# W_up for two pairs: 26 quarter-block products in place of seven half-block ones

## The chip, the cores and the metric

The kernel runs on one core of a Trainium2 chip. TensorE (PE) multiplies matrices into PSUM, eight banks of 512 f32 values for each of 128 partitions; VectorE (DVE), ScalarE (ACT) and GpSimd (POOL) work element by element, and SyncE (SP) issues DMAs. The metric is the device time of one execution in microseconds, as a median over runs.

## The reference

Input x is 128 samples of 64 channels by 1024 positions, f32. Two residual layers:

```python
x = x + ffn0(cond0(x))       # cond0: a 64x64 channel mix per sample, mixed from 8 kernels by an attention
                             # ffn0: out = in @ (A @ B.T).T + bias, rank 128
y = cond1(x)                 # grouped convolution over 1024 positions, 9 taps, 4 groups, plus a context
logits = y @ gate_w.T + expert_bias        # 4 experts
base   = einsum("bth,oh->bto", y, W_up)    # 1024 x 1024: most of the arithmetic
delta  = one_hot(argmax(logits)) picks one of 4 rank-8 LoRA products of y
x = x + base + delta
```

The 8192 rows (128 samples x 64 channels) each take a 1024 x 1024 product with `W_up`, all in f32.

## The kernel before

**Tiling.** Two samples make a *pair*: 128 rows by 1024 columns, tile `x` (64 pairs). Two pairs make a *group* `d` (32 groups), pair a = 2d and pair b = 2d+1. The convolution's result comes out transposed, as `yt` (128 positions by [2 pairs, 8 chunks, 128 rows]), so a 128x128 piece of `yt` is the stationary matrix of a matmul and a piece of `W_up` the moving one. PSUM: a pool `ps` of four banks (tags `bank`) for all small steps, and four banks `pb0` to `pb3` for W_up.

**W_up before.** With a0, a1 (b0, b1) the halves of pair a (b) along the 1024 inputs, and 11, 12, 21, 22 the four 512x512 blocks of W_up, seven block products do for eight. `product()` (L459) makes one: four matmuls of 512 columns. `ffn_sums` (L478) makes four sums of `yt` blocks on POOL; `w_sum` (L137) makes T1, T2, T3, -T4 from the weight blocks once, on DVE. `ffn_a` (first product, copied to SBUF as `v` by ACT), `ffn_second`, `ffn_both`, `ffn_b`, `ffn_hi` and `ffn_last` make the products; DVE makes `u2`, `u3` out of PSUM (L549, L558), POOL adds them to `x` (L550, L551, L559), DVE adds T1's product to `x` (L564). `lora` (L586) puts the four expert results onto the open banks and one bank `pl`; `results` (L594) adds them to `x` with four DVE additions, and SP stores the two `x` tiles.

**Order.** All five engines run in the order in which the program names the work (a manual schedule); waits on semaphores are put in from the data. For group d of the main loop (L735) PE does: `layer0_out(2d+5)` (two matmuls `pd` of 512 columns, added to `x` by DVE at L353; `x` goes through DRAM, `x1d`, and comes back as `X`), `gate` (L506, matmul `pgt`, then eight small DVE operations L514 to L526), the last five products of group d with `turn` (`pzt`) among them, then `tiles`: `shared_in` (`pm`), `gate_in` (`pg`, for group d+1), `conv_in` (`pc`, for group d+2), `lora`; then `layer0_in` of the two pairs 2d+6 and 2d+7 (`pxb`), `layer0_mix` (`pz`), the first product of group d+1, `layer0_out(2d+6)`, `layer0_mix`, the second product. So the `yt` that group d+1 needs was complete one turn earlier.

**POOL's order** in a turn: `add_fbias` of two pairs (L603), the three additions to `x`, `differences` of two pairs (L389, L390), the loads of two later pairs (`load_x`, two DMAs each, L108, L109), then `ffn_sums(d+1)`.

**The start.** Before the loop, lines L636 to L734 do the conditioning, load the weights (L673 to L677), run pairs 0 to 5 through layer 0 and group 0's products up to `ffn_hi`, with the weight sums between them:

```python
gate_out(0, gate_in(0)); ffn_sums(0); add_fbias(4, nc.gpsimd)      # L700 to L702
ffn_a(0); layer0_in(4)
w_sum("T1", "12", "11"); w_sum("T2", "22", "T1"); w_sum("T3", "22", "12")
```

Of the kernel before, what the change touches and what calls it, by code (L numbers as in the profile page):

```python
# [52 lines left out]
E, R = 4, 8  # L53
ER = E * R
GL = E + ER
HC = NC // 2
H = P // 2
N = 512
GT = 64
NX = 3  # L60
NBD = 3
FIRST = 4
PLAIN = 2

PK = tuple(np.cumsum([0, P, P, 1, 1, P, 8, 8, CH, CH, E]).tolist())

# [2 lines left out]
def block(ctx: ExitStack, tc: tile.TileContext, a: dict, out: bass.AP):  # L69
# [21 lines left out]
    def bank(name):  # L91
        return ps.tile([P, 512], F32, tag="bank", name=name)
# [35 lines left out]
    load_x(0, nc.sync)  # L128
    at = loaded("AT", [P, L])
    wk = loaded("wk", [P, 8, 2, CH], eng=nc.scalar)  # L130
    W = {}

    def load_w(name, eng, tag=None):
        W[name] = const.tile([P, HC, N], F32, tag=tag or f"w{name}", name=f"w{name}")
        eng.dma_start(W[name], a[f"w{name}"])

    def w_sum(name, x, y):  # L137
        W[name] = const.tile([P, HC, N], F32, tag=f"w{name}", name=f"w{name}")
        nc.vector.tensor_tensor(W[name], W[x], W[y], ALU.subtract)


    X = []
# [110 lines left out]

    def own_bias(pr):

        mv[pr] = const.tile([8, 2, CH], F32, name=f"mv{pr}")
        for b in range(2):
            nc.scalar.activation(mv[pr][:, b], bk, AF.Copy, scale=attT[:8, 2 * pr + b : 2 * pr + b + 1])

    def own_bd(pr):  # L260
        bdx[pr] = const.tile([P, 2, CH], F32, name=f"bdx{pr}")
        for k in range(8):
            w = attx[pr][:, k : k + 1]
            if k == 0:
                nc.vector.tensor_scalar(bdx[pr], wk[:, k], w, None, ALU.mult)
            else:
                nc.vector.scalar_tensor_tensor(bdx[pr], wk[:, k], w, bdx[pr], ALU.mult, ALU.add)  # L267
# [22 lines left out]
    def agg_all():  # L290

        to = aggd.rearrange("b i o -> b (i o)").rearrange("b (j h n) -> h b j n", j=4, h=2)
        for h in range(2):
            pool, tag = ((const, "wT3"), (ytp, "yt"))[h]
            agg = pool.tile([NB, 4, 512], F32, tag=tag, name=f"agg{h}")
            aggs.append((to[h], agg))
            ps4 = [spare(j, f"pagg{h}_{j}") for j in range(4)]
            for j in range(4):
                rows = slice(32 * j, 32 * (j + 1))
                nc.tensor.matmul(ps4[j], attT[rows, :], wa[rows, h], start=True, stop=True)  # L300
            for j in range(4):
                if j % 2:
                    nc.scalar.copy(agg[:, j], ps4[j])
                else:
                    nc.vector.tensor_copy(agg[:, j], ps4[j])
            yield

    def agg_out():
# [3 lines left out]

    lo, hi = slice(0, N), slice(N, L)
    xbs, z0s, yts, opened = {}, {}, {}, {}
    diffs, pms, m2s, pcs, zgs, vs, ss, u2s = {}, {}, {}, {}, {}, {}, {}, {}

    def layer0_in(pr):
        xt = xts.pop(pr)
# [137 lines left out]
            conv_in(pr, b)  # L456
            conv_out(pr, b)

    def product(to, yt, w, first=True):  # L459

        for c in range(HC):
            nc.tensor.matmul(  # L462
                to, yt[:, c], w[:, c], start=first and c == 0, stop=c == HC - 1, skip_group_check=not first
            )

    def halves(d):

        yt = yts[d]
        return [[yt[:, t, h * HC : (h + 1) * HC] for h in range(2)] for t in range(2)]

    def ffn_a(d):

        opened[d] = [psb.tile([P, N], F32, tag=f"pb{i}", name=f"pb{i}_{d}") for i in range(4)]
        product(opened[d][0], halves(d)[0][0], W["11"])
        vs[d] = sums.tile([P, N], F32, tag="v", name=f"v{d}")
        nc.scalar.copy(vs[d], opened[d][0])

    def ffn_sums(d):  # L478
        (a0, a1), (b0, b1) = halves(d)
        s = [sums.tile([P, HC, P], F32, tag=f"s{i}", name=f"s{i}_{d}") for i in range(4)]  # L480
        nc.gpsimd.tensor_tensor(s[0], b0, b1, ALU.add)
        nc.gpsimd.tensor_tensor(s[1], s[0], a0, ALU.subtract)
        nc.gpsimd.tensor_tensor(s[2], a0, b0, ALU.subtract)
        nc.gpsimd.tensor_tensor(s[3], a1, s[1], ALU.subtract)
        ss[d] = s

    def gate_in(d):

# [49 lines left out]
        nc.scalar.copy(zt, p[:, :P])  # L538
        return zt

    def ffn_second(d):
        product(opened[d][0], halves(d)[0][1], W["21"], False)

    def ffn_both(d):

        xa, xb = xs[2 * d], xs[2 * d + 1]
        product(opened[d][1], ss[d][1], W["T2"])
        u2s[d] = sums.tile([P, N], F32, tag="u2", name=f"u2_{d}")
        nc.vector.tensor_tensor(u2s[d], opened[d][1], vs.pop(d), ALU.add)  # L549
        nc.gpsimd.tensor_tensor(xa[:, hi], xa[:, hi], u2s[d], ALU.add)  # L550
        nc.gpsimd.tensor_tensor(xb[:, lo], xb[:, lo], u2s[d], ALU.add)  # L551

    def ffn_b(d):

        xb = xs[2 * d + 1]
        product(opened[d][2], ss[d][2], W["T3"])
        u3 = sums.tile([P, N], F32, tag="u3", name=f"u3_{d}")
        nc.vector.tensor_tensor(u3, opened[d][2], u2s.pop(d), ALU.add)  # L558
        nc.gpsimd.tensor_tensor(xb[:, hi], xb[:, hi], u3, ALU.add)  # L559

    def ffn_hi(d):
        xb = xs[2 * d + 1]
        product(opened[d][3], ss[d][0], W["T1"])
        nc.vector.tensor_tensor(xb[:, hi], opened[d][3], xb[:, hi], ALU.add)  # L564

    def ffn_last(d, zm):
        p, s = opened[d], ss.pop(d)
        zt = turn(d, zm)
        product(p[2], halves(d)[1][1], W["-T4"], False)
        product(p[3], s[3], W["22"], False)  # L570
        del yts[d]
        return zt

    def ffn(d):

        zm = gate(d)
        ffn_both(d)
        if 2 * d + 4 < NPAIR:
            differences(2 * d + 4)
        ffn_b(d)  # L580
        if 2 * d + 5 < NPAIR:
            differences(2 * d + 5)
        ffn_hi(d)
        return ffn_last(d, zm)

    def lora(d, zt):  # L586

        p = opened[d]
        p.append(bank(f"pl{d}"))
        for j, i in enumerate((0, 3, 2, 4)):  # L590
            rows = slice(j * ER, (j + 1) * ER)
            nc.tensor.matmul(p[i], zt[rows, :], lb[rows, :], start=i == 4, stop=True, skip_group_check=i < 4)  # L592

    def results(d):  # L594
        p = opened.pop(d)
        xa, xb = xs.pop(2 * d), xs.pop(2 * d + 1)
        for x, cols, part in ((xa, lo, p[0]), (xa, hi, p[3]), (xb, lo, p[2]), (xb, hi, p[4])):
            nc.vector.tensor_tensor(x[:, cols], part, x[:, cols], ALU.add)  # L598
        nc.sync.dma_start(out[2 * d], xa)
        nc.sync.dma_start(out[2 * d + 1], xb)  # L600

# [68 lines left out]
    load_context(1)  # L670
    gl = loaded("gl", [P, NC, GT], eng=nc.scalar)
    lb = loaded("lb", [P, N], eng=nc.scalar)
    layer0_out(1, lambda: load_w("11", nc.sync))  # L673
    load_x(4, nc.sync)
    load_w("21", nc.sync)
    load_w("12", nc.sync, tag="w-T4")
    load_w("22", nc.sync)  # L677
    wsum = const.tile([P, NGC, P], F32, tag="sel", name="wsum")
    nc.gpsimd.tensor_tensor(wsum, ws[:, :, 0], ws[:, :, 1], ALU.add)
    add_fbias(3, nc.gpsimd)  # L680
# [17 lines left out]
    conv(1)  # L698

    gate_out(0, gate_in(0))  # L700
    ffn_sums(0)
    add_fbias(4, nc.gpsimd)  # L702
    ffn_a(0)
    layer0_in(4)
    w_sum("T1", "12", "11")
    w_sum("T2", "22", "T1")
    w_sum("T3", "22", "12")
    ffn_second(0)
    zm = gate(0)
    ffn_both(0)  # L710
    ffn_b(0)
    differences(2)
    layer0_mix(4)
    layer0_out(4, lambda: load_x(6, nc.sync))
    w_sum("-T4", "21", "T2")
    ffn_hi(0)
    add_fbias(5, nc.gpsimd)
    differences(3)
    layer0_in(5)
    layer0_mix(5)  # L720
    back5 = layer0_out(5, lambda: load_x(7, nc.sync), later=True)
    shared_in(2)
    back5()
    shared_in(3)
# [10 lines left out]
    for d in range(NPAIR // 2):  # L735
        more = d + 1 < NPAIR // 2
        ahead = [pr for pr in (2 * d + 6, 2 * d + 7) if pr < NPAIR]
        if d and 2 * d + 5 < NPAIR:
            layer0_out(2 * d + 5)
        if 2 * d + 5 < NPAIR:  # L740
            load_context(d + 2)
        if ahead:
            load_cond(d + 3)
        for pr in ahead:
            add_fbias(pr, nc.gpsimd)
        if d:
            zt = ffn(d)
        else:
            differences(4)
            differences(5)  # L750
            zt = ffn_last(0, zm)
        tiles(d, zt, 2 * d + 4, 2 * d + 5)
        for pr in (2 * d + 8, 2 * d + 9):
            if pr < NPAIR:
                load_x(pr)
        if more:
            ffn_sums(d + 1)
        for pr in ahead:
            layer0_in(pr)
        if ahead:  # L760
            layer0_mix(ahead[0])
        if more:
            ffn_a(d + 1)
        if ahead:
            layer0_out(ahead[0])
            layer0_mix(ahead[1])
        if more:
            ffn_second(d + 1)


def _by_rows(v):
# [101 lines left out]
```

## Time and profile before

| | |
|---|---|
| median of 3 runs (lowest, highest) | 1336.34 us (1336.19, 1337.31) |
| the profiled execution's own time | 1338.59 us |
| its span | 1336.8 us, mean granted TensorE clock 0.998 |
| busy | PE 1317.1 us (99%), weight loads 759.3, POOL 616.5 (46%), DVE 552.8 (41%), ACT 139.0 (10%) |
| DMA | 189.37 MB, 142 GB/s |

A matmul in f32 shows as two records, so 512 columns are `x2`. Records of PE overlap each other (their mean duration is longer than their spacing); the time that one takes in a stream is read from the chain of waits, which gives the length of a stretch and the records in it. POOL and DVE records are durations of single instructions. The page's engine shares are means over a start of some 100 us, 30 equal turns and an end of some 60 us with less in it.

### The profile page before, as it was taken

Reading aid. Unit: us, or ns where it says so; the run is one execution under the profiler, and the core shown is the slowest. Engines: PE = TensorE matmul, PEld = TensorE weight load, DVE = VectorE, ACT = ScalarE, POOL = GpSimd, SP = SyncE. Lnnn points to the kernel's source line nnn. Section 1 sums busy time; section 2 is a strip of 40 time slices with the busy share of each in tenths; the row PEclk is TensorE's granted clock in tenths of the full one; section 3 lists DMA queues with packets and bytes.
Section 4 is the critical chain, followed back from the end, with each engine's and each line's share of the span. In section 5 each row is a group of like instructions: output and inputs, shape, how many; then the busy total and the mean of one; then the engine's idle time right before and its main releaser. Section 6 shows DMA issues by size and latency. Waiting matters only on the chain.

```text
span 1336.8 us, 18273 instructions
## 1 busy us (share of the span) xinstructions
PE 1317.1 (99%) x7303; PEld 759.3 (57%) x7303; DVE 552.8 (41%) x978; ACT 139.0 (10%) x310; POOL 616.5 (46%) x541
## 2 busy tenths in 40 slices
PE   8899999999999999999999999999999999999997
PEld 6565565655665555665555655555656556656543
DVE  6652443433443423444424434324434334434222
ACT  2010111110111010111000111101111101111100
POOL 2465534455443455443555343555343555435321
PEclk9999999999999999999999999999999999999999
DMA  9965544345544455534455434455444455433301
GB/s 313 317 158 169 152 142 134 106 137 167 151 137 123 108 152 167 149 122 128 106 167 153 153 126 113 127 167 152 142 134 107 136 167 152 142 119 96 78 32 63
DMA packets 183845, 189.37 MB, mean 142 GB/s; under 512 B 17361, under 2 KB 156625, under 8 KB 183249
## 3 DMA queue, kind: packets, MB, share of 16 engines
q1 hardware_dynamic: 166480, 125.81, 33.7%
q0 software_dynamic: 16128, 58.73, 13.2%
q10 hardware_dynamic: 1152, 3.67, 0.8%
q8 instruction: 58, 0.95, 0.3%
q14 instruction: 27, 0.21, 0.1%
HBM read 118.90 MB, written 69.27 MB: 141 GB/s over the span
## 4 chain that ended last, share of the span: by engine, by line
PE 96%; DVE 2%; DMA 1%; issue 0%; ACT 0%; SPq 0%; DVEq 0%; ACTq 0%
PE pb L462 58%; PE pxb L321 9%; PE pd L352 8%; PE pc L435 8%; PE pm L397 4%; PE pg L493 4%; PE pb L592 2%; PE pz L331 1%; PE pgt L511 1%; DMA x<-in_x 1%; DVE bdx L267 1%; DMA xt<-in_xt 0%; DVE yt L447 0%; PE pc L426 0%; PE pzt L536 0%
## 5 line engine op out<-in xcount | busy, mean ns | idle before, releaser
L462 PE MATMUL pb<-wT,s 128*128 128x512 f32 x768 | 337.6, 596 | 0.0
L109 POOL DMA_DIRECT2D x<-in_x x56 | 29.5, 528 | 494.9 <-DVE z L339 428.2
L462 PEld LDWEIGHTS pb<-wT,s 128*128 128x128 f32 x768 | 143.5, 190 | 168.4 <-issue 168.4
L462 PE MATMUL pb<-w,yt 128*128 128x512 f32 x512 | 230.8, 593 | 3.1 <-DVE x L598 1.7
L353 DVE TENSOR_TENSOR x<-pd,x 128x512 f32<-128x512 f32 x128 | 88.4, 691 | 236.4 <-PE pd L352 235.9
L412 DVE TENSOR_TENSOR m<-pm,cx 64x512 f32<-64x512 f32 x124 | 85.4, 689 | 219.4 <-PE pm L397 216.5
L603 POOL TENSOR_TENSOR x<-x,ffn_bias 128x1024 f32<-128x1024 f32 x62 | 146.8, 2387 | 34.2 <-DMA x<-in_x 34.2
L462 PEld LDWEIGHTS pb<-w,yt 128*128 128x128 f32 x512 | 92.4, 190 | 98.6 <-issue 92.2
L321 PEld LDWEIGHTS pxb<-B,xt 128*128 128x128 f32 x1024 | 119.8, 195 | 25.2 <-DVE yt L447 22.0
L447 DVE TENSOR_TENSOR yt<-pc,m 128x512 f32<-128x512 f32 x124 | 121.3, 1099 | 20.8 <-ACT m L415 20.1
L352 PE MATMUL pd<-AT,z 128*128 128x512 f32 x256 | 122.4, 599 | 5.2 <-DVE yt L447 1.8
L321 PE MATMUL pxb<-B,xt 128*128 128x128 f32 x1024 | 125.6, 281 | 0.0
L462 PE MATMUL pb<-w-T,yt 128*128 128x512 f32 x256 | 115.2, 592 | 0.0
L462 PE MATMUL pb<-w,s 128*128 128x512 f32 x256 | 115.1, 592 | 0.0
L435 PE MATMUL pc<-ws,df 128*64 128x128 f32 x1984 | 113.6, 273 | 0.0
L435 PEld LDWEIGHTS pc<-ws,df 128*64 128x64 f32 x1984 | 110.4, 137 | 4.3
L550 POOL TENSOR_TENSOR x<-x,u 128x512 f32<-128x512 f32 x32 | 40.4, 1264 | 144.6 <-DVE u L549 144.6
L415 ACT COPY m<-m 64x512 f32<-64x512 f32 x124 | 76.5, 617 | 265.4 <-DVE m L412 261.9
L352 PEld LDWEIGHTS pd<-AT,z 128*128 128x128 f32 x256 | 48.2, 191 | 65.3 <-issue 57.4
L462 PEld LDWEIGHTS pb<-w,s 128*128 128x128 f32 x256 | 48.6, 190 | 61.2 <-issue 61.2
L462 PEld LDWEIGHTS pb<-w-T,yt 128*128 128x128 f32 x256 | 46.2, 190 | 54.8 <-issue 54.8
L397 PEld LDWEIGHTS pm<-wsum,X 128*64 128x64 f32 x992 | 53.7, 138 | 23.5 <-issue 23.5
(110 smaller groups left out, 1136.0 us busy)
## 6 DMA issues: line engine op xcount, KB each, us to landing
x1d<-x SPq DMA_DIRECT2D x128, 256.0 KB, 3.4
X<-x1d SPq DMA_DIRECT2D x128, 256.0 KB, 4.3
out<-x SPq DMA_DIRECT2D x64, 512.0 KB, 2.6
xt<-in_xt POOLq DMA_DIRECT2D x56, 512.0 KB, 4.5
x<-in_x POOLq DMA_DIRECT2D x56, 512.0 KB, 4.1
cx<-ctxd SPq DMA_DIRECT2D x32, 128.0 KB, 4.3
w<-in_w SPq DMA_DIRECT2D x4, 1024.0 KB, 9.5
ab<-aggbd SPq DMA_DIRECT2D x30, 128.0 KB, 3.2
```

Source lines behind the costliest of these rows:

```text
L321: nc.tensor.matmul(pxb[:, :P], xt[:, c, :], bt[:, c, :], start=(c == 0), stop=(c == NC - 1))
L352: nc.tensor.matmul(pd, z0, at[:, cols], start=True, stop=True)
L353: nc.vector.tensor_tensor(x[:, cols], pd, x[:, cols], ALU.add)
L397: nc.tensor.matmul(pm[b * H : (b + 1) * H, g * P : (g + 1) * P], blocks(pr, b, g, 1), wsum[:, g], start=True, stop=True,)
L412: nc.vector.tensor_tensor(by_group(m2[half, b]), by_group(pm[half]), context(pr, b, half), ALU.add)
L415: nc.scalar.copy(m2[other, b], m2[half, b])
L435: nc.tensor.matmul(pc[o * H : (o + 1) * H, cols], diffs[pr][:, 2 * g + b, o], ws[:, g, o], start=True, stop=True,)
L447: nc.vector.tensor_tensor(yt.rearrange("m q (o g two) -> m two g q o", two=2, g=NGC)[:, b], by_group(pcs.pop((pr, b))), context(pr, b) if ...
L462: nc.tensor.matmul(to, yt[:, c], w[:, c], start=first and c == 0, stop=c == HC - 1, skip_group_check=not first)
L493: nc.tensor.matmul(pg[rows, : 2 * P].rearrange("m (t r) -> m t r", t=2), gl[:, c, :], yt[:, :, c], start=c < 2, stop=c >= NC - 2,)
L550: nc.gpsimd.tensor_tensor(xa[:, hi], xa[:, hi], u2s[d], ALU.add)
L603: eng.tensor_tensor(xs[pr], xs[pr], fbias, ALU.add)
```

## The change

W_up for a group is now computed by another bilinear algorithm. `yt` of the two pairs is cut into eight blocks (2 pairs x 4 quarters of the inputs, two chunks of 128 each), W_up into 16 blocks of 256 inputs x 256 outputs, and the results into eight *parts* of 256 columns: part r is half r % 2 of bank `pb{r // 2}`, and results part r belongs to pair r // 4, columns 256 (r % 4). Thirty-two block products would be the plain way; here 26 do, named P0 to P25 below in the order of `PRODUCTS`. A product is two matmuls of 256 columns.

Before them, 17 sums of `yt` blocks are made for every group, on POOL (s0 to s16, by `Y_SUMS`, 256 columns each), and 31 sums of weight blocks once, on DVE (by `W_SUMS`, 512 columns each, in place in 26 slots). A row of `PRODUCTS` is (part, `yt` block or sum, weight slot, flag of the first matmul in a bank, number of weight sums that must be made by then, what is done with the part after the product). Values are handed from part to part, while the part goes on accumulating: "copy" is an ACT copy from PSUM into PSUM, with the sign; "add" is an ACT copy to SBUF (`v`) and a DVE addition into PSUM; "dcopy" is a DVE copy in PSUM; "x" is a DVE addition of the part to (or subtraction from) the `x` tile. A group has 14 "x", three "add", one "dcopy" and six "copy". PE waits for hand-ons by whole banks.

POOL no longer adds to `x`. `lora` uses the four open banks and no fifth; `results` adds in the order pb1, pb3, pb2, pb0, and SP issues the stores as before, pair a's ahead of pair b's. In the loop, the products of group d+1 are P0 to P3 and P4 to P7 where the first and second product stood, and P8 to P22, `turn`, P23 to P25 follow the gate; `differences` come ahead of all products; `ffn_sums(d+1)` stands before `load_x` on POOL. At the start, `add_fbias(4)` comes before `ffn_sums(0)`, and the 31 weight sums are spread over group 0's products. Some small tiles share memory with others (`agg0` becomes two tiles and two stores).

```diff
-HC = NC // 2
+QC = NC // 4
+NQ = N // 2
+Y_SUMS = (
+    (4, "+", 5), (0, "-", 8), (9, "+", 1), (2, "-", 10), (4, "-", 7), (0, "-", 12), (3, "-", 13),
+    (2, "+", 14), (6, "-", 15), (16, "-", 5), (12, "-", 15), (17, "-", 18), (11, "-", 8), (20, "-", 19),
+    (21, "+", 7), (7, "-", 13), (21, "+", 3),
+)
+W_SUMS = (
+    (10, 8, "-", 10), (16, 10, "-", 6), (17, 4, "n", 16), (2, 2, "-", 6), (18, 11, "-", 15),
...
+)
+PRODUCTS = (
+    (2, 6, 8, 1, 0, (("copy", 0, "-"),)),
+    (4, 10, 17, 1, 3, (("x", 4, "+"),)),
+    (6, 11, 16, 1, 3, (("copy", 1, "+"),)),
+    (2, 12, 2, 0, 4, (("x", 6, "+"),)),
+    (6, 2, 19, 0, 6, (("add", 0, "+"),)),
+    (5, 8, 3, 0, 7, (("add", 4, "-"),)),
+    (3, 17, 21, 0, 10, (("x", 7, "+"), ("x", 1, "+"))),
+    (0, 15, 18, 0, 11, (("x", 7, "+"),)),
+    (5, 5, 1, 0, 12, (("x", 7, "-"),)),
+    (7, 8, 10, 0, 15, ()),
+    (7, 19, 5, 0, 15, (("x", 1, "+"), ("x", 5, "+"))),
+    (2, 13, 20, 0, 16, (("x", 2, "+"),)),
+    (1, 20, 6, 0, 16, (("x", 2, "-"),)),
+    (4, 9, 22, 0, 17, (("add", 2, "-"),)),
+    (6, 18, 15, 0, 17, (("copy", 7, "-"), ("copy", 3, "-"))),
+    (1, 21, 23, 0, 18, (("copy", 6, "-"),)),
+    (4, 1, 7, 0, 19, (("x", 1, "-"), ("x", 3, "+"))),
+    (2, 0, 24, 0, 21, (("dcopy", 4, "+"), ("x", 0, "+"))),
+    (6, 22, 9, 0, 22, (("x", 5, "-"),)),
+    (0, 14, 25, 0, 23, (("copy", 2, "+"),)),
+    (4, 23, 0, 0, 25, ()),
+    (6, 7, 4, 0, 27, ()),
+    (1, 10, 10, 0, 27, ()),
+    (1, 24, 13, 0, 28, ()),
+    (7, 16, 11, 0, 30, ()),
+    (2, 3, 12, 0, 31, ()),
+)
...
+        for r, u, w, new, _, then in PRODUCTS[first:end]:
+            p = part(d, r)
...
+            for c in range(QC):
+                nc.tensor.matmul(
+                    p, ys[d][u][:, c], W[:, w, c], start=new == 1 and c == 0, stop=c == QC - 1, skip_group_check=True
+                )
+            for kind, to, op in then:
...
+                elif kind == "add":
+                    copy = sums.tile([P, NQ], F32, tag="v", name=f"v{d}_{to}")
+                    nc.scalar.copy(copy, p)
+                    combine(nc.vector, part(d, to), part(d, to), op, copy)
...
     gate_out(0, gate_in(0))
+    add_fbias(4, nc.gpsimd)
     ffn_sums(0)
...
+    def first_products(n):
+        end = done[0] + n
+        w_sums(PRODUCTS[end - 1][4])
+        products(0, done[0], end)
...
+    first_products(4)
     layer0_in(4)
+    first_products(4)
     zm = gate(0)
+    first_products(4)
     layer0_mix(4)
     layer0_out(4, lambda: load_x(6, nc.sync))
     add_fbias(5, nc.gpsimd)
+    differences(2)
+    first_products(4)
+    layer0_in(5)
     differences(3)
+    first_products(3)
     layer0_mix(5)
     back5 = layer0_out(5, lambda: load_x(7, nc.sync), later=True)
+    first_products(3)
...
         if d:
+            products(d, 8, 23)
...
+        zt = turn(d, zm)
         if d:
+            products(d, 23, 26)
...
         tiles(d, zt, 2 * d + 4, 2 * d + 5)
+        if more:
+            ffn_sums(d + 1)
         for pr in (2 * d + 8, 2 * d + 9):
             if pr < NPAIR:
                 load_x(pr)
...
         if more:
+            products(d + 1, 0, 4)
         if ahead:
             layer0_out(ahead[0])
             layer0_mix(ahead[1])
         if more:
+            products(d + 1, 4, 8)
```

## The prediction

> **What bounds the kernel now.** I read the page's busy times first, then the chain of waits through one turn of the loop, then the rows of single instructions, then the timeline of the start and the end.
>
> ```profile
> PE 1317.1 (99%) x7303; PEld 759.3 (57%) x7303; DVE 552.8 (41%) x978; ACT 139.0 (10%) x310; POOL 616.5 (46%) x541
> PE 96%; DVE 2%; DMA 1%; issue 0%; ACT 0%; SPq 0%; DVEq 0%; ACTq 0%
> ...
> 640.95 10.38 PE pb L462 x24
> 651.33 0.11 PE pzt L536
> 651.44 6.87 PE pb L462 x16
> 658.31 1.90 PE pm L397 x32
> 660.21 1.73 PE pg L493 x16
> ...
> 666.50 3.77 PE pxb L321 x32
> 670.27 0.22 PE pz L331 x2
> 670.50 3.44 PE pb L462 x8
> 673.93 1.72 PE pd L352 x4
> 675.65 0.22 PE pz L331 x2
> 675.87 3.44 PE pb L462 x8
> ```
>
> TensorE is never idle in this turn; each piece begins where the last ends, and W_up (`pb`) takes 10.38 + 6.87 + 3.44 + 3.44 = 24.13 us of 41. So a turn shortens by what PE saves, as long as nobody else comes late. Idle PE is found only in the start (the windows up to 80 us) and the end.
>
> **Loop: the products.** Removed per group: 56 records of 512 columns, 24.13 us (430 ns each). Added: 26 x 2 matmuls = 104 records of 256 columns. The nearest row is `pg`, the only one that streams 256 columns: 16 records, two of them at a time side by side, 1.73 us, so 216 ns per step. 104 x 216.25 ns = 22.49 us: 1.64 us saved a group, 50.8 us over the 31 groups of the loop. Its weights are 64 wide, here they are 128 wide. With 128 wide weights the trace has 128 columns (`pxb`, 3.77/32 = 117.8 ns) and 512 (430 ns); the line between them gives 222 ns at 256, 23.08 us, 1.05 us a group, 32.5 us. Half a 512-record, 215 ns, gives 22.36 us, 54.9 us. I take 216, since `pxb` shows loads and streams together passing every 118 ns, far inside 216; 222 and 215 stay as ends.
>
> The Trainium skill speaks against it: "TensorE: Matmul & The Clock Gate", Part 3, The mechanism, lets a weight load overlap a running matmul only where the row groups differ, and its section on LDWEIGHTS gives 107 ns for 128 columns. All row groups are used here, so by that rule, an estimate from that page, a record costs 213 + 107 ns and the change loses 3.4 us a group, 105 us in all. The 430 ns spacing of the 512-column records contradicts it.
>
> **Loop: the hand-ons.** Each value handed on is a wait of PE for ACT or DVE. What one costs in the open is shown at the end of the run, where PE had nothing else:
>
> ```profile
> 1302.73 1.89 DVE L598 TENSOR_TENSOR x<-pb,x 128x512 f32<-128x512 f32 x3 [9.16 <-PE pl L592]
> 1303.48 3.70 PE L462 MATMUL pb<-w,yt 128*128 128x512 f32 x8 [0.77 <-DVE x L598]
> ...
> 1307.22 0.58 ACT L476 COPY v<-pb 128x512 f32<-128x512 f32 x1 [5.15 <-PE pb L462]
> 1307.86 3.70 PE L462 MATMUL pb<-w,yt 128*128 128x512 f32 x8 [0.68 <-ACT v L476]
> ```
>
> The bracket is PE's idle time: 0.68 us through ACT, 0.77 through DVE, for 512 columns. For 256, an ACT copy falls from 0.585 to 0.361 (`zg`, L504), so 0.46; a DVE operation out of PSUM takes 0.691 for 512 columns (L353) and 0.344 for 128 (L339), on the line between them 0.46, so 0.55. The tables leave at least two products, 1.73 us, between a hand-on and its use: P0 to P3, P12 to P15, P13 to P16, P17 to P20, P18 to P21, P19 to P22 by one engine, P4 to P7 by both (1.01). All stay under 1.73 with 0.7 or more over. The queue ahead of P4's addition: DVE's `z` would end at 676.63 and `v` come at 677.15, so nothing is before it. No PSUM-to-PSUM copy is in the trace: bounds 0.36 and 0.585 (the 512 row), still covered. Price taken: 0; in the open, ten such hand-ons would be 5 us a group.
>
> One queue is nearer. P8's subtraction stands on DVE behind the eight gate operations, and P13 waits for its bank, 5 x 0.865 = 4.33 us after `pgt`. The gate takes 2.2 us at 681.4; in the turn shown it took 4.1, because one 8-column operation lasted 2.27 us (minimum 0.166, means 0.65 and 0.36 for L518 and L519). Then P13 is 0.2 us late. I put 1.5 us for all turns (0 to 9, a 0.3 in each).
>
> **Loop: DVE, ACT, POOL, queues.** DVE gets 18 operations of 0.46 for three of 0.69: +6.2 us a turn, 41% to about 56%, hidden in its idle time before L353 and L412 (236 and 219 us). ACT gets some 3.1 us more, 10% to 18%. POOL: a 256-column sum is 0.70 us (1.264 for 512, 2.387 for 1024), 17 make 11.9, in place of 5.3 + 3.8: +2.8 us. s2 must wait for P22 of the group before; from there PE has P23 to P25, `pm`, `pg`, `pc`, `lora`, `pxb`, `pz` and P0, some 15.8 us to P1; fifteen sums at 0.70 to 0.78 take 11.7. Hidden; if POOL came late, each us would be on PE's path. `load_x` is moved behind the sums: its `x` loads wait for the store of an earlier pair anyhow (POOL idles 17.2 us there, until 671.1), and the stores come 1.2 us later, since the first now waits for the fourth addition of `results`, not the second. The bias additions and `differences` queued behind these loads have a turn of slack. X for `pm` lands at 645.4 + 4.3 = 649.7, `pm` starts near 656.7: 7 us left. Zero for all of these.
>
> **The start.** Here DVE is on the path.
>
> ```profile
> 49.81 2.27 DVE L139 TENSOR_TENSOR wT<-w,w 128x2048 f32<-128x2048 f32 x1
> 50.05 3.17 POOL L481 TENSOR_TENSOR s<-yt 128x512 f32<-128x512 f32 x1 [15.83 <-DVE yt L447]
> 51.90 3.70 PE L462 MATMUL pb<-w,yt 128*128 128x512 f32 x8
> 52.12 3.24 DVE L139 TENSOR_TENSOR wT<-w,wT 128x2048 f32<-128x2048 f32 x1
> 53.29 3.20 POOL L482 TENSOR_TENSOR s<-s,yt 128x512 f32<-128x512 f32 x1
> ```
>
> A POOL sum that takes 1.27 us elsewhere takes 3.2 here, and DVE's 3.24: SBUF-to-SBUF operations of the two take turns. So a weight sum of 512 columns is 2.27/4, about 0.6 us, and 0.6 + 0.75 = 1.35 while POOL makes its sums. 31 weight sums are 18.6 us bare, against four that measured 11.4. Laid out by these rows: P0 at 52 as now; P1 waits for s2 (53.8), P3 for s4 (56.0); `pxb` to 58.8; sums 5 to 11 alternate with POOL and end at 66.8, P7 at 68.3; gate, with POOL's bias addition in the way, to 73; five weight sums to 76; P11 ends at 78.2; `pz`, `pd` and DVE's additions to 81.7; two sums, P15 ends at 85; four sums in `pxb`'s shadow, P18 at 89.5; second `pd` 92.2; five sums to 96.1, P21 at 97.1. `pm` and `pc` then end at 102.5, the convolution's DVE additions 2.5 us later, the last four sums at 107.4, P25 at 108.7. Before, group 0 was done at 92.2: **+16.5 us**. Ends: the bare extra DVE time less PE's own gain, +5; all 31 at 1.35, 42 - 11.4 - 1.6 = +29.
>
> **The end.** Both stores follow the fourth addition: +0.3 for the issue, up to 1.3 if two 512 KB stores share the engines (2.6 us each): +0.7. The first banks' waits in the last groups (0.77 + 0.68) stay about the same.
>
> **Sum.** -50.8 + 1.5 + 16.5 + 0.7 = -32.1 us. The profiled execution took 1338.59 us with a span of 1336.8; it lies 2.25 over the median. I carry the difference to the median: 1336.34 - 32.1 = 1304.
>
> **Rivals.**
> *Hand-ons in the open.* Many short waits, if PSUM-to-PSUM operations or the bank waits are slower than their rows. For: none such was ever run here. Against: 0.7 us to spare. At 0.5 us a group: 1304 + 15.5 = 1320.
> *Slower: weight loads stick out.* A load lasts 190 ns and now has 216 instead of 430 to hide in. For: 26 ns over. Against: `pxb`'s 118. The gain is used up by the start at a record of (24.13 - 0.60)/104 = 226 ns. At 236 ns W_up takes 24.54: 31 x 0.41 + 18.7 = +31, 1368.
> *A cheap start.* If DVE gets ahead of POOL: +5, 1293.
> *A dear start with records of 222 ns:* -32.5 + 29 + 2.2, 1335.
>
> **How the numbers follow.** Forecast 0.60 (its own range 1295 to 1312); hand-ons in the open 0.17 (1312 to 1333); cheap start 0.07; dear start and slow records 0.04 (half of it inside 0.2%, 2.7 us, about what can be told from no change); weight loads or POOL late, slower, 0.12. The range 1289 (54.9 saved, start +8) to 1334 leaves out the slower case and little else. Faster 0.84, same 0.03, slower 0.13.
>
> **What would show it.** Right: a turn of 39.7 us in the chain, products of P8 to P22 as one stretch near 12.98 us (x60), PE without idle in the loop, the first `tiles` of the loop some 16 us later, DVE near 56% and POOL near 53%. Wrong: PE waits on ACT or DVE at the product line, records over 222 ns, a loop in which POOL's s sums release PE, or a start that costs under 8 or over 25 us.

## The result and the profile after

The changed kernel takes 1313.06 us (median; 1312.16 to 1314.66) beside 1336.82 us of the kernel before on the same chip: a ratio of 0.9823, with a 95% interval of 0.9806 to 0.984. The forecast was 1304, its range 1289 to 1334. The profiled execution took 1312.86 us with a span of 1311.1, 25.7 less than the span of before. Two marks split these 25.7 into three stretches: the start of `pm` for pairs 4 and 5, where group 0 is done, and the end of the last `lora`:

| stretch, us | before | after | difference | predicted |
|---|---|---|---|---|
| span's start to `pm` of pairs 4, 5 | 92.22 | 114.51 | +22.3 | +16.5 |
| from there to the end of the last `lora` | 1238.1 | 1188.9 | -49.2 | -49.3 |
| from there to the span's end | 6.45 | 7.7 | +1.2 | +0.7 |
| sum | | | -25.7 | -32.1 |

From the page of the kernel after, the busy times, the granted clock over the span, the chain by engine and the two rows of W_up's matmuls:

```profile
PE 1275.2 (97%) x8839; PEld 1054.2 (80%) x8839; DVE 734.3 (56%) x1485; ACT 226.2 (17%) x566; POOL 727.9 (56%) x861
...
PEclk9889999999999999999999999999999999999999
...
PE 93%; DVE 3%; DMA 2%; issue 0%; ACT 0%; SPq 0%; DVEq 0%; ACTq 0%
...
L538 PE MATMUL pb<-w,s 128*128 128x256 f32 x2432 | 562.9, 382 | 12.1 <-DVE w L196 9.1
...
L538 PE MATMUL pb<-w,yt 128*128 128x256 f32 x896 | 229.6, 385 | 8.0 <-DMA w<-in_wq 2.6
```

PE is still the bound, but for 97% of the span. Weight loads rose from 759 to 1054 us, DVE from 41% to 56%, and all that PE idles at W_up's line (12.1 and 8.0 us) is small against 1275. The clock digit drops in the second and third slices, at 33 to 98 us. From the chain of waits of the kernel after, one turn (start, length, what):

```profile
643.06 0.37 PE pgt L583 x4
643.43 13.03 PE pb L538 x60
...
656.57 2.59 PE pb L538 x12
...
671.34 3.46 PE pb L538 x16
...
676.74 3.46 PE pb L538 x16
...
682.27 7.85 PE pb L538 x36
```

Every piece, those left out here too, is PE's and begins where the last one ends: none of the ten hand-ons of a group holds it. The products take 13.03 + 2.59 + 3.46 + 3.46 = 22.54 us instead of 24.13: 104 records at 217 ns, 1.59 us saved a group, and 31 x 1.59 = 49.3. A turn is 682.27 - 643.43 = 38.84 us. The waits of PE in the kernel after (who waited for whom: us in total, times, longest), first from 46 to 115 us, then, the last line, from 115 us to the end:

```profile
PE pb L538 <- DVE w L196: 11.6, 7, 3.5
PE pb L538 <- DVE w L194: 3.6, 3, 1.9
PE pb L538 <- DMA w<-in_wq: 2.6, 1, 2.6
...
PE pb L538 <- DVE x L623: 2.1, 4, 1.0
```

So PE waits for the weight sums in the start (15.2 us in ten waits), and in the 1196 us behind it only 2.1 us, where a group's first records wait for the `results` of the one before at the end of the run. The timeline of the start (start, length, engine, line, instructions in it; the bracket is idle time before it and who ended it):

```profile
69.43 7.77 DVE L196 TENSOR_TENSOR w<-w 128x512 f32<-128x512 f32 x5
69.62 2.70 POOL L629 TENSOR_TENSOR x<-x,ffn_bias 128x1024 f32<-128x1024 f32 x1 [7.74 <-DMA x<-in_x]
70.26 2.05 PE L538 MATMUL pb<-w,yt 128*128 128x256 f32 x4 [2.56 <-DVE w L196]
72.28 1.49 POOL L450 TENSOR_TENSOR df<-X 128x512 f32<-128x512 f32 x1
...
75.81 4.87 PE L538 MATMUL pb<-w,s 128*128 128x256 f32 x12 [3.50 <-DVE w L196]
...
107.68 4.44 DVE L196 TENSOR_TENSOR w<-w 128x512 f32<-128x512 f32 x4
```

Five weight sums take 7.77 us where POOL adds a bias and makes differences beside them, the last four 4.44. The x12 row behind the 3.50 us wait (P9 to P11) lasts 4.87 us, where twelve records of the loop take 2.59 by the chain. The chain of waits of the start holds this stretch and two more like it, P1 to P3 and P24 with P25:

```profile
54.72 5.18 PE pb L538 x12
...
75.81 4.89 PE pb L538 x12
...
111.03 3.47 PE pb L538 x8
```

The windows of the kernel after say why (stretch, its length, busy us and records of PE, weight loads, DVE, ACT, POOL, then the granted clock, the DMA share and GB/s):

```profile
50.00:60.00 10.00, 6.43 (x19) 5.02 (x20) 4.52 (x6) 0.72 (x2) 9.37 (x12) 0.66 0.92 320
60.00:70.00 10.00, 5.98 (x35) 4.87 (x34) 9.16 (x22) 1.01 (x3) 2.26 (x4) 0.98 0.99 212
70.00:80.00 10.00, 6.24 (x14) 4.52 (x15) 7.81 (x8) 0.00 (x0) 8.10 (x5) 0.50 0.06 10
```

PE was granted a clock of 0.66 and 0.50 in the first and the last; in the kernel before both had 1.00. PE's idle share alone does not tell it, since the stretch between, as idle as the others, had 0.98. In finer windows the clock is 0.50 from some 52.7 to 59.2, 69.7 to 79.5 and 110.6 to 114.0 us. PE had waited from 48.99 to 51.64, from 67.70 to 70.26, and from 106.5 to 108.5 and 109.6 to 111.0: the low clock sets in late in a wait or just behind it and lasts into the next products.

### The profile page after: what moved, and what is told of

The parts are those of the page before. It is cut to its first block, busy times and chain, and to the rows that moved or that the text cites. A ratio compares the mean times of both kernels' runs of the same rounds, so it can differ in the third digit from the quotient of the medians.

```text
span 1311.1 us, 22851 instructions
## 1 busy us (share of the span) xinstructions
PE 1275.2 (97%) x8839; PEld 1054.2 (80%) x8839; DVE 734.3 (56%) x1485; ACT 226.2 (17%) x566; POOL 727.9 (56%) x861
## 4 chain that ended last, share of the span: by engine, by line
PE 93%; DVE 3%; DMA 2%; issue 0%; ACT 0%; SPq 0%; DVEq 0%; ACTq 0%
PE pb L538 55%; PE pxb L382 9%; PE pd L413 8%; PE pc L496 8%; PE pm L458 4%; PE pg L565 4%; PE pb L617 3%; DVE w L196 1%; PE pz L392 1%; DMA w<-in_wq 1%; PE pgt L583 1%; DVE yt L508 0%; DVE x L623 0%; DMA X<-x1d 0%; DMA x1d<-x 0%
## 5 line engine op out<-in xcount | busy, mean ns | idle before, releaser
L538 PE MATMUL pb<-w,s 128*128 128x256 f32 x2432 | 562.9, 382 | 12.1 <-DVE w L196 9.1
L538 PEld LDWEIGHTS pb<-w,s 128*128 128x128 f32 x2432 | 461.8, 192 | 83.1 <-DVE w L196 11.5
L538 PE MATMUL pb<-w,yt 128*128 128x256 f32 x896 | 229.6, 385 | 8.0 <-DMA w<-in_wq 2.6
L538 PEld LDWEIGHTS pb<-w,yt 128*128 128x128 f32 x896 | 164.0, 192 | 29.3 <-DVE x L623 3.4
L450 POOL TENSOR_TENSOR df<-X 128x512 f32<-128x512 f32 x62 | 65.3, 1054 | 214.7 <-DMA X<-x1d 200.1
L555 DVE TENSOR_TENSOR x<-pb,x 128x256 f32<-128x256 f32 x320 | 126.9, 418 | 99.2 <-PE pb L538 94.6
L196 POOL TENSOR_TENSOR s<-yt,s 128x256 f32<-128x256 f32 x224 | 164.8, 736 | 17.8 <-PE pb L538 2.8
L382 PEld LDWEIGHTS pxb<-B,xt 128*128 128x128 f32 x1024 | 119.0, 194 | 23.8 <-DVE yt L508 22.0
L196 POOL TENSOR_TENSOR s<-s,yt 128x256 f32<-128x256 f32 x128 | 94.3, 737 | 16.3 <-PE pzt L608 9.0
L196 POOL TENSOR_TENSOR s<-s,s 128x256 f32<-128x256 f32 x128 | 92.2, 731 | 5.0
L557 DVE SCALAR_TENSOR_TENSOR x<-pb,x 128x256 f32<-128x256 f32 x128 | 53.9, 421 | 64.4 <-PE pb L538 61.3
L157 POOL DMA_DIRECT2D x<-in_x x56 | 29.5, 528 | 108.5 <-DMA out<-x 86.0
```

The source lines that it names most:

```text
L196: eng.tensor_tensor(to, x, y, ALU.add if op == "+" else ALU.subtract)
L382: nc.tensor.matmul(pxb[:, :P], xt[:, c, :], bt[:, c, :], start=(c == 0), stop=(c == NC - 1))
L450: nc.gpsimd.tensor_tensor(diffs[pr][:, :, 0], at_even, at_odd, ALU.subtract)
L538: nc.tensor.matmul(p, ys[d][u][:, c], W[:, w, c], start=new == 1 and c == 0, stop=c == QC - 1, skip_group_check=True)
L555: nc.vector.tensor_tensor(x, p, x, ALU.add)
```

## The experiments

**Records of 256 columns alone.** The kernel before, with each matmul of W_up as two of 256 columns:

```diff
-            nc.tensor.matmul(
-                to, yt[:, c], w[:, c], start=first and c == 0, stop=c == HC - 1, skip_group_check=not first
-            )
+            for n in range(2):
+                cols = slice(n * N // 2, (n + 1) * N // 2)
+                nc.tensor.matmul(
+                    to[:, cols],
+                    yt[:, c],
+                    w[:, c, cols],
+                    start=first and c == 0 and n == 0,
+                    stop=c == HC - 1,
+                    skip_group_check=True,
+                )
```

> The kernel before, its seven block products kept, but each matmul of 512 columns made as two of 256 with the same weights loaded twice: 112 records a group in place of 56, no hand-on added. Theory (256 columns stream at 216 ns a record, loads hidden): 24.2 us a group in place of 24.1, +3 us in all, near 1340. Rival (each record costs some ns more, hidden in the changed kernel by something else): at 222 ns 24.9 us a group, +23 us.

Measured: 1341.51 us, 1.004 of before (1.0025 to 1.0055). Its chain of waits, the four stretches of W_up in a turn:

```profile
642.40 10.44 PE pb L464 x48
...
652.95 6.91 PE pb L464 x32
...
672.04 3.46 PE pb L464 x16
...
677.43 3.46 PE pb L464 x16
```

Together 24.27 us for 112 records, 216.7 ns each, against 24.13 for 56 of 512 columns: 0.14 us a turn, 4.5 us in 32. Twice as many loads of 128 wide weights cost the loop nothing more. The 222 ns of the line between `pxb` and 512 columns fall, and so does the slower rival's record over 226 ns. The Trainium skill ("TensorE: Matmul & The Clock Gate", Part 3, The mechanism) lists weight loads as overlapping a running matmul only when the row groups differ, by which a load with all row groups in use would not overlap; here it does, at every record. The same section also has loads into the background weight buffer pulled ahead, with which the measurement agrees.

**A hand-on in the open.** P22, which waits for P19's copy, moved next to P19 so that no product stands between:

```diff
     (0, 14, 25, 0, 23, (("copy", 2, "+"),)),
+    (1, 10, 10, 0, 27, ()),
     (4, 23, 0, 0, 25, ()),
     (6, 7, 4, 0, 27, ()),
-    (1, 10, 10, 0, 27, ()),
```

> P22 stands right behind P19, whose ACT copy reads P22's bank; P20 and P21 follow. Nothing else changes. Theory (hand-ons cost nothing in the changed kernel only because two products stand between): the hand-on is now open and costs 0.46 us in each of 31 turns, +14 us, near 1327, and the turn is 39.3 us. Rival (a hand-on is hidden or nearly free wherever it stands): under +3 us.

Measured: 1335.86 us, 0.9993 of before (0.9984 to 1.0003): 22.8 us over the changed kernel, nearly its whole gain. From its waits of PE (whole span) and its chain of one turn:

```profile
PE pb L538 <- ACT pb L545: 14.3, 32, 0.4
```
```profile
652.34 10.45 PE pb L538 x48
...
662.82 0.37 ACT pb L545
...
663.23 2.86 PE pb L538 x12
```

The wait is 0.45 us, as foretold from the end of the run (0.46). It costs more than that: the twelve records behind it take 2.86 us instead of 2.59. Together that is 0.72 us a turn, and 22 us in 31 turns; 14 were expected. This tells apart a zero that was covered from one that was cheap anyway: with the products between them the hand-ons are hidden; one of ten left open takes back the gain.

**POOL's order.** The loads of later pairs put ahead of the sums again, as in the kernel before:

```diff
-        if more:
-            ffn_sums(d + 1)
...
+        if more:
+            ffn_sums(d + 1)
```

> Undoes one move: on POOL the loads of the two later pairs stand ahead of the 17 sums again. Theory (the sums are hidden only because they stand before the loads, which wait for a store): the store of the first pair is issued at about 670 and lands 3.5 us later, the three DMA issues behind it take 1.6 us, s2 is done near 677.4 where P1 would start at 672.2: 5 us in each of the 28 turns with loads, +140 us or more, 1450. Rival (POOL's place does not matter, it has half its time free): under +10 us.

Measured, in one execution: 1558.4 us, span 1556.6, mean clock 0.933. Its waits of PE (whole span), and its chain of waits in one turn:

```profile
PE pb L538 <- POOL s L196: 143.7, 28, 6.3
PE pb L538 <- DVE x L557: 27.5, 27, 1.2
```
```profile
647.83 2.65 DMA out<-x
...
651.02 0.53 POOL x L157
...
652.61 0.74 POOL s L196
...
655.00 5.12 PE pb L538 x12
```

A store holds POOL's load (L157), the loads hold the sums, and PE stands about 5 us a turn. The first records behind the wait run at 427 ns, so the idle time costs clock as well; the 245 us are more than the 171 that these two waits add up to, and the expectation, 140 or more, lay far below. The move is what lets POOL's 17 sums be hidden at all: in the changed kernel a turn has 15 sums at 0.73 us between P22 and P1, and PE never waits for them.

**No weight sums.** The 31 sums left out, so the products use the 16 raw weight blocks, without further slots, and the results are not the reference's:

```diff
-        for to, x, op, y in W_SUMS[wdone[0] : upto]:
+        for to, x, op, y in ():
...
-                    p, ys[d][u][:, c], W[:, w, c], start=new == 1 and c == 0, stop=c == QC - 1, skip_group_check=True
+                    p, ys[d][u][:, c], W[:, w % 16, c], start=new == 1 and c == 0, stop=c == QC - 1, skip_group_check=True
```

> Leaves out the 31 weight sums; every product takes the raw weight block whose number is the slot modulo 16. All products, hand-ons and sums on POOL stay. Theory (the start is dear because PE waits for DVE's weight sums, 11.6 + 3.6 us by the list of waits, and POOL loses time to them): group 0 is done 15 to 19 us sooner than at 114.5, span 1292 to 1296 us; the loop is unchanged, 38.84 us a turn. Rival (the start is dear by hand-ons, by the sums on POOL or by the loads): less than 6 us sooner.

Measured, in one execution: 1284.9 us, span 1283.1. `pm` of pairs 4 and 5 starts at 86.88, 27.6 us before that of the changed kernel, and from there to the span's end it is 0.4 us shorter (1196.2 and 1196.6). So the sums cost 27.6 us, all of it in the start, with the waits and the low clock that come with them: here the granted clock is 1.00 from 40 to 87 us. Without them group 0 is done 5.3 us sooner than in the kernel before, which made four sums itself. Theory (15 to 19) and rival (under 6) had both put this lower.

**POOL's sums of group 0 left out** (raw blocks in their place, so group 0's results are not the reference's):

```diff
+        if d == 0:
+            ys[0] = [yts[0][:, t, QC * k : QC * (k + 1)] for t in range(2) for k in range(4)] * 4
+            return
```

> Leaves out POOL's 17 sums of group 0 (its products take raw blocks of yt); the 31 weight sums stay. In the changed kernel the 31 weight sums took 28.9 us of DVE where 31 at their shortest (0.68) take 21.1, since POOL's sums, a bias addition and differences take turns with them. Theory (turn-taking is a term of its own): the first eleven sums, 9.6 us there, take 7.5, the start is 1 to 4 us shorter, the rest stays with the bias addition and the differences. Rival (the sums' number alone sets the start): no change, within 1 us.

Measured, in one execution: 1307.9 us, span 1306.1; `pm` of pairs 4 and 5 at 109.23, 5.3 us sooner, more than the theory's 1 to 4. The first weight sums in the chains of waits, of the changed kernel and of this one:

```profile
51.62 0.70 DVE w L196
52.35 1.11 DVE w L196
```
```profile
52.43 0.70 DVE w L196
53.16 0.70 DVE w L196
```

A sum of 512 columns takes DVE 0.70 us alone and 1.10 while POOL makes its sums, and the first eleven take 7.6 us instead of 9.6, as the theory had it. That DVE and POOL lengthen each other's work is shown by taking POOL's away. But by the end of the gate only 1.8 of the 5.3 us are gained (67.76, not 69.51). The rest is won behind it, since P9 starts at 70.59, 5.2 us sooner. From this run's chain:

```profile
67.76 0.61 DVE w L196
...
68.50 2.05 PE pb L541 x4
...
70.59 4.81 PE pb L541 x12
```

POOL's bias addition waits for the load of pair 5's `x`; it began at 71.56 and not at 69.62. The five sums behind the gate were done before it and took 3.46 us instead of 7.77. Where this addition and the differences behind it fall against the five sums is thus worth some 4 us of the start.

**The order of the weight loads.** Quarter 2, which P0 needs, first instead of last:

```diff
-    layer0_out(1, lambda: load_w(3, nc.sync))
+    layer0_out(1, lambda: load_w(2, nc.sync))
...
-    for k in range(3):
+    for k in (1, 0, 3):
```

> The weight quarter that P0 needs (slots 8 to 11) is loaded first instead of last. In the changed kernel PE stood 2.65 us before P0 for it (51.64), and DVE began its weight sums with it at 51.62. Theory (the late weights are one term of the dear start): P0 and the first sums begin at about 49, 2 to 2.6 us earlier, median near 1310.7. Rival (a later meeting sets the start: the bias addition of pair 5 on POOL begins only when its x lands, at 69.6, and the five weight sums after it take turns with it): less than 1 us is left of the gain.

Measured: 1312.95 us, 0.9824 of before (0.9803 to 0.9845), the same as the changed kernel. P9 starts 3.2 us sooner (72.56, not 75.81), P15 ends 2.5 us sooner (85.14, not 87.68), but `pm` of pairs 4 and 5 starts only 1.05 sooner (113.46), and that ends level. From its chain:

```profile
72.56 5.49 PE pb L538 x12
...
113.46 3.11 PE pm L458 x32
```

What the earlier weights gain is lost again to a lower clock: P9 to P11 take 5.49 us instead of 4.89, P20 and P21 3.42 from start to end instead of 2.37, P24 and P25 3.78 instead of 3.47, and `pm`'s 32 records 3.11 instead of 1.90. The granted clock of 90 to 100 us was 0.83, where the changed kernel had 1.00. So the late weights are on the path as far as P15; the rival's number came true (nothing is left at the end), but its reason, POOL's bias addition, does not account for the loss.

**PE kept busy.** Idle matmuls ahead of P1, P8, P9, P23 and P24 of group 0, where PE waits, to keep the clock up:

```diff
+        waits = {1: 6, 8: 8, 9: 12, 23: 6, 24: 4} if d == 0 else {}
...
+            if k in waits:
+                busy(bank(f"idle{k}"), waits[k])
```

> The changed kernel with dummy 128-column matmuls on PE in group 0, ahead of the products that wait longest for weight sums: 6 before P1, 8 before P8, 12 before P9, 6 before P23, 4 before P24, some 0.24 us each, less than the wait. In the changed kernel the granted clock of 70 to 80 us was 0.50 and P9 to P11 took 4.89 us for 12 records in place of 2.6. Theory (idle PE also loses its clock, and that is 5 to 7 us of the dear start): the clock stays at 1.00 there and 4 to 6 us are gained, 1307 to 1309. Rival (the slow records are only late sums): no gain, or a loss by the dummies.

Measured: 1311.0 us, 0.9812 of before (0.9797 to 0.9826), not told apart from the changed kernel; 4 to 6 us were expected. From its windows and its chain:

```profile
70.00:80.00 10.00, 6.50 (x45) 5.97 (x45) 7.90 (x13) 0.00 (x0) 4.92 (x5) 1.00 0.00 0
```
```profile
75.27 2.68 PE idle L260 x24
77.95 2.61 PE pb L543 x12
```

From 70 to 80 us the clock is back at 1.00, and P9 to P11 take 2.61 us instead of 4.89. Yet they end at 80.6, where those of the changed kernel end at 80.7, and `pm` of pairs 4 and 5 comes only 1.4 us sooner (113.13). What the clock is worth does not follow from this, since two other things came late in this execution. POOL's bias addition began at 68.13 and not at 69.62, beside the gate, which ended at 72.9 instead of 69.5. And the 24 idle matmuls ran until 77.95, while the sum that P9 needs was made by 76.8, so they held P9 themselves. Idle matmuls in these places gain some 2 us, if anything, and what the low clock costs stays open.

**Group 0 by plain products.** Thirty-two raw block products for group 0, so that no weight sum stands before its end; the sums lie beside it and go on into group 1's first products. The weight quarters are loaded in the order of their use. Three versions differ in where the sums are put (the number is how many are made by then):

```diff
+    def plain(k, first=False):
+        for r in range(8):
+            for c in range(QC):
+                nc.tensor.matmul(
+                    part(0, r),
+                    yts[0][:, r // 4, QC * k + c],
+                    W[:, 4 * k + r % 4, c],
+                    start=first and r % 2 == 0 and c == 0,
+                    stop=c == QC - 1,
+                    skip_group_check=True,
+                )
...
-    first_products(4)
+    plain(2, True)
+    w_sums(3)
...
-    first_products(4)
+    plain(0)
...
+    w_sums(12)
+    plain(1)
...
+    w_sums(20)
+    plain(3)
...
+            w_sums(26)
...
+        w_sums(31)
```

> Group 0 alone is computed by 32 plain block products without sums or hand-ons, quarter by quarter of the inputs, and the 31 weight sums follow each quarter on DVE beside the next one, the last five before group 1. Loads in the order of use. Theory (the start is dear since each sum stands between two products in the same stretch): PE pays 32 instead of 28 blocks, group 0 is done some 4 to 9 us after the kernel before, not 22, and the median is 1296 to 1301. Rival (DVE's 21 us of sums must be paid wherever they stand): they hold up group 1 instead, and less than 5 us is gained, over 1308.

The second spreads the sums further into group 1:

```diff
-    w_sums(12)
+    w_sums(8)
...
+            w_sums(31)
...
-            w_sums(26)
...
-        w_sums(31)
+        w_sums(22)
...
+        w_sums(25)
...
+        w_sums(28)
```

> As e6_plain0, with the weight sums placed in smaller pieces behind the DVE operations that PE waits for: three after the first quarter, five after pair 4, twelve after pair 5, and the last eleven between the products of group 1. In e6_plain0 PE stood 5.0 us for a context addition and 3.0 for z behind sums. Theory (the sums cost PE nothing where no such operation is queued behind them): 8 to 12 us less than e6_plain0, 1291 to 1296. Rival (DVE is short of time there, whatever the order): 1301 or more.

The third keeps these places, with more of the sums in the earlier ones:

```diff
-    w_sums(8)
+    w_sums(12)
...
-    w_sums(20)
+    w_sums(24)
...
-            w_sums(31)
...
-        w_sums(22)
+        w_sums(26)
...
-        w_sums(25)
+        w_sums(29)
...
-        w_sums(28)
+        w_sums(31)
```

> As e8_plain0_spread, with the weight sums earlier: twelve after pair 4, twelve after pair 5, two after group 0's results, three after P3 and two after P7 of group 1, none behind the gate. In e8 PE stood 3.97 us before P13 of group 1, for P8's subtraction that was queued behind three sums and the gate, and its next 12 records took 5.49 us in place of 2.6 at a lower clock. Theory (that queue is what is left of the sums): 4 to 7 us less than e8, 1293 to 1296. Rival (DVE has no room left in group 1): under 2 us.

Measured (the ratio to before with its interval; `pm` of groups 0 and 1 from the timelines, us):

| | time | ratio | `pm`, group 0 done | `pm`, group 1 done | span |
|---|---|---|---|---|---|
| changed kernel | 1313.06 | 0.9823 (0.9806 to 0.984) | 114.4 | 153.3 | 1311.1 |
| plain group 0 | 1303.19 | 0.9745 (0.9722 to 0.9768) | 98.4 | 145.4 | 1303.3 |
| spread | 1299.27 | 0.9713 (0.9691 to 0.9735) | 96.3 | 142.6 | 1300.2 |
| early | 1298.51 | 0.9699 (0.9683 to 0.9715) | 101.1 | 141.3 | 1298.8 |

All three beat both kernels, and the spans follow the column of group 1. The longest wait of PE for DVE in the start of each, plain, spread and early in this order:

```profile
PE pc L496 <- DVE m L473: 5.0, 1, 5.0
```
```profile
PE pb L538 <- DVE x L557: 4.0, 1, 4.0
```
```profile
PE pd L413 <- DVE z L400: 4.9, 2, 4.5
```

One wait of 4 to 5 us stays and moves. With the sums late, PE waits in group 1 (P13's first record, at 128 us, for P8's subtraction from `x`; the clock of 125 to 140 us falls to 0.77); with them early, in group 0: `z` of layer 0 stands on DVE behind sums, one of which lasts 2.85 us beside a bias addition of POOL. From the early version's chain:

```profile
77.60 2.85 DVE w L194
...
81.65 0.27 DVE z L400
...
81.97 3.78 PE pd L413 x4
```

What the early version wins in group 1 (6.1 us) it loses first in group 0 (4.8), so the last two are not told apart. All three fell 2 to 3 us short of what was expected of them, and the last step, 0.8 us, is what its rival had (under 2). Whether an order of the sums without such a wait exists was not tried.

## Why the prediction was right, and where it was off

- **The loop: right.** 217 ns a record were taken as 216, 1.59 us a group as 1.64. The record of 256 columns with its 128 wide load, run by itself, gave 216.7. That the table has -49.2 beside -49.3 is partly luck: 1.5 us too much saved by the records, and 1.5 us set aside for P13 that were not needed.
- **The hand-ons at zero: right, and for the reason given.** Two products cover them. What one costs in the open was undersized: 0.46 us was its wait alone, and the 0.27 us by which the twelve records behind it are longer lay outside the bracket that the estimate was read from. The rival of hand-ons in the open, 0.5 us a group, did not come.
- **P13's wait, 1.5 us for all turns: too much.** PE does not wait there in the loop.
- **DVE, ACT and POOL beside PE: right in size** (56%, 17% and 56%, taken as 56, 18 and 53; a POOL sum 0.735 us, taken as 0.70 to 0.78). The move of the pairs' loads behind the sums was priced at zero, and it costs nothing; but only what it might lose was considered. Without it the change would have lost over 200 us.
- **The turn was misread.** 41 and 39.7 us were named as the turns before and after; by the chains they are 40.44 (640.95 to 681.39) and 38.84. The sum did not use them.
- **The start: the term that was mis-sized, 22.3 us and not 16.5.** The layout held up to P0 (52.0 laid out, 51.6 measured) and P7 (68.3 and 67.2). Then two errors met and partly cancelled, which is luck. The gate was laid out to 73 with POOL's bias addition in its way; it ended at 69.5, since the addition came behind it. The five weight sums, laid out as 3 us, met that addition and the differences and took 7.77: done at 77.2 instead of 76. P11 ended 3.5 us behind them instead of 2.2, since PE ran at the low clock: at 80.7 instead of 78.2. Up to P21 (100.0 instead of 97.1) only 0.4 us more were added. The last four sums took 4.4 us, not 2.4, since POOL's differences and group 1's sums ran beside them: the layout had turn-taking only with group 0's sums. P25 ended 2.4 us behind the last of them instead of 1.3, again at the low clock (3.47 us for eight records): at 114.5 instead of 108.7. So counted, the rows of sums cost some 3.2 us of the 5.8 and PE behind them some 2.4. A bare sum is 0.68 us, not 0.6: a row of 2048 columns divided by four is too short for one of 512, and 31 x 0.68 is 21.1, not 18.6; all 31 took 28.9 us. The clock was not considered at all. The kernel with idle matmuls makes the three slow stretches of the chain 2.61, 2.61 and 2.26 us long instead of 5.18, 4.89 and 3.47; if all of that lay on the path, the clock would cost 6 us.
- **The end:** +1.2 us, taken as +0.7. The two stores are issued at 1305.93 and 1306.31.
- **From the profiled execution to the median.** The sum was made against a profile of before that lay 2.25 us over its median, and the 32.1 us were carried to the median. From profile to profile the change is -25.7, from median to median -23.8. Of the 8.8 us by which the median missed the forecast, 6.4 are in the table and 2.4 come from this.

Shown: the size of the record, the price of an open hand-on, that the weight sums with the waits and the low clock they bring cost 27.6 us and all of it in the start, that DVE and POOL lengthen each other's sums, and that earlier weights or idle matmuls alone leave the median where it was. Not settled: what the low clock costs, up to 6 us. Argued only: how the 5.8 us over the forecast divide between the sums and the clock.

## What to carry to other kernels

An algorithm with fewer products pays on a bound PE only if its one-time sums stay off the path: do the first group the plain way while they are made, which gave another 10 to 15 us here. Put at least two products (1.73 us here) between a value handed on and its use, and look at every in-order queue for a DMA wait that the new work would stand behind. Price a one-time stretch by instructions of the size that it issues, beside the other engine's whole queue in that stretch, not only the part that changes, and read there what the idle time does to PE's clock.

## What the runs showed of the hardware that was not expected

- A matmul of 256 f32 columns with a new 128 wide weight load each costs 216 to 217 ns a record, half of the 430 of 512 columns: the load (190 to 192 ns) is hidden wholly.
- An exposed hand-on in PSUM (256 columns through ACT) costs 0.45 us of waiting and 0.27 us in the twelve records behind it.
- With waits of PE of 2.65 and 2.56 us, and with two of 1.9 and 1.45 us 1.1 us apart, the granted clock fell to 0.50 for 3 to 10 us, and records of 256 columns took 0.41 to 0.43 us. Idle matmuls in the waits kept 50 to 60 and 70 to 80 us at 1.00.
- A sum of two SBUF operands of 512 columns takes DVE 0.69 us alone, 1.10 us beside POOL's sums, 1.42 beside its differences and up to 2.85 beside its bias addition. The Trainium skill ("SBUF — State Buffer", Who interferes with whom) has DVE operations with two SBUF inputs contend with POOL's reads; the run without POOL's sums, where the same instructions took 0.70, agrees.
